# Summing a token's expert rows on TensorE, and layer 3 as one chain of stages per half of the tokens

## The chip, the core and the metric

The kernel runs on one core of a Trainium2 chip. The core has a matrix engine (TensorE; PE in the profile, PEld for its weight loads), a vector engine (VectorE, DVE), a scalar engine (ScalarE, ACT), a general engine (GpSimd, POOL), a queue for transfers (SyncE, SP) and 16 DMA engines. Each engine works through its own instructions in a fixed order and waits on semaphores for the others. Products land in PSUM, in eight banks; everything else lies in SBUF or in device memory. The metric is device microseconds for one execution.

## What is computed

The reference is a stack of four layers on 1024 tokens (x, 4 x 256 x 256, float32). Every layer is a feed-forward, an attention and the same feed-forward again, each on the normalized x and added to x. What matters here are layers 2 and 3:

```python
x = x + 0.5 * _L2_ffn_ref(_layernorm(x, axis=-1), ...)
x = x + _L2_attn_ref(_layernorm(x, axis=-1), ...)
x = x + 0.5 * _L2_ffn_ref(_layernorm(x, axis=-1), ...)
x = x + 0.5 * _L3_ffn_ref(_layernorm(x, axis=-1), ...)
x = x + _L3_attn_ref(_layernorm(x, axis=-1), ...)
x = x + 0.5 * _L3_ffn_ref(_layernorm(x, axis=-1), ...)
```

The feed-forward of layer 2 has 64 experts and a shared part. A token goes to its best six experts, and its output is the sum of their six rows and of the shared product:

```python
topk_w, topk_idx = jax.lax.top_k(scores, K)                    # K = 6 of E = 64
gx = xp[buf_tok]                                               # the tokens of each expert
hid = jax.nn.silu(g) * u                                       # gate and up, 96 wide
eo = jnp.einsum('ech,ehi->eci', hid, down_proj) * buf_w[..., None]
routed = jnp.zeros((T + 1, h), x.dtype).at[buf_tok.reshape(-1)].add(eo.reshape(-1, h))[:T]
shared = jax.nn.silu(xf @ shared_gate_w.T) * (xf @ shared_up_w.T) @ shared_down_w.T
return (routed + shared).reshape(b, s, h)
```

Layer 3's feed-forward is `relu(x @ w_up + b_up) @ w_down + b_down`, 256 to 1024 to 256. Its attention works on each of the four sequences of 256 tokens by itself: 16 query heads and 4 key heads with a rotary position, 16 tokens compressed into one key and one value by a softmax, a softmax of each query over the 16 compressed keys, and an output projection. Layer 3's feed-forward works token by token, so no token of one sequence needs another sequence.

## The kernel before

x stays in SBUF as eight tiles of 128 tokens (`m.x[0..7]`); tiles 0 to 3 are half 0 (two sequences), 4 to 7 half 1. `norm` (L165) makes statistics of each tile of a half on DVE (L172, L173), one inverse root for four tiles in a chain of 14 small DVE operations (`rsqrt`, L155 to L163), the normalized tile (`xn`, L180), two transposes per tile on PE with the identity (L136), and a copy into `xT[half]`, by turns on DVE (L142) and ACT (L144). `mm` (L132) is every chain of products, `add_to_x` (L204) adds a scaled result to x on DVE.

The program is written out in one order of tracing. A planner of the framework then orders each engine's instructions: it runs through its own simulated time, and each engine takes, of those instructions whose inputs are ready there, the one that was traced first. Where nothing is late the order on an engine is thus the order of tracing. Buffers of one name are handed out in rotation, in the order of tracing. A pool opened where an earlier pool lay waits until that one is free.

**Layer 2's feed-forward**, `l2_ffn`, is called twice, before and after layer 2's attention. It normalizes all eight tiles and then makes lists of tokens for the experts, mostly on DVE. In the second call `beside()` follows, which decodes layer 3's weights (PE, ACT, POOL). Then 16 groups of four experts run, up to eight at a time (`staggered`). A group gathers its tokens with two indirect transfers by POOL (L977, ten buffers named rows), transposes them, multiplies by gate and up (L996), makes h (L1006), multiplies by down and scatters the rows by two more indirect transfers by POOL (L1025) into `parts` in device memory, one row for each token and choice. The experts' weights come by SP in eight loads of gate and up and four of down, into six slots in the first call and five in the second. After the groups the shared part is traced: `gated` (L188 to L201) makes gate and up products of a half, 96 wide, into mmb banks, SiLU on ACT (L196) and the product on DVE (L198), and the down product of each tile goes to x (L204). Last, each tile of 128 tokens loads its 6 x 256 numbers per token from `parts` (`got`, L1043, four buffers, which waits for all scatters), POOL adds three of the six rows to the other three (L1049), and DVE adds the three to x (L204 again).

**Layer 3** is made of two generators, each of which traces a step and yields. `l3_ffn` (L1559) normalizes a half, adds the bias to x on POOL (L1563), yields, makes eight products of 512 columns (up, with ReLU by turns on ACT and DVE, L1572 and L1570) and yields after each, and then makes four tiles of the down product, each added to x. `l3_attn` (L1626) normalizes a half and then runs its two sequences in turns, the second three steps behind the first; a sequence has 18 steps, of products, rotary operations (L1646 on DVE, L1647 on POOL), two softmaxes (L1603 to L1610) and transposes. Both use mmb (four banks), trb (two) and accb (two). The main program runs the feed-forward of half 0 alone; then the attention of half 0 beside the feed-forward of half 1, two steps of attention to one of feed-forward; then the attention of half 1 beside the second feed-forward of half 0, in the same way; then the second feed-forward of half 1 alone. At the end SP stores each tile (L1793).

## Time and profile before

| | us |
|---|---|
| median of 14 runs | 2105.07 (2095.1 to 2111.15) |
| the profiled execution | 2095.62, its span 2093.9 |
| first layer-2 feed-forward: experts and their sums (first gather to the first product of the attention behind it) | 878.9 to 1006.6 |
| second layer-2 feed-forward: the same, to the first up-product of layer 3 | 1772.2 to 1894.3 |
| layer 3, first up-product to last add | 1894.3 to 2091.2 |
| busy: PE, DVE, ACT, POOL | 1815.4, 1199.3, 708.1, 577.7 |

Times are counted from the start of the span, in us. A line of a group or of the time line gives the engine, the line of the kernel, the operation, the tile written and the tiles read (`x<-got,x`), and the shape. What stands in square brackets is the time for which the engine had been idle, and what ended that. "x12924" counts instructions; a product of float32 is two records, each with a weight load. In the answers by stretches the columns are the length, the busy time and number of records of PE, PEld, DVE, ACT and POOL, the granted clock of TensorE as a share of its full speed, the mean share of the 16 DMA engines and GB/s.

### The profile page before, as it was taken

How to read it: one execution, taken by the hardware profiler on the slowest of the kernel's cores; microseconds unless marked ns; L12 is line 12 of the kernel's file. 1: busy time of each engine (PE TensorE's matmuls, PEld its weight loads, DVE VectorE, ACT ScalarE, POOL GpSimd, SP SyncE). 2: the span in 40 equal slices, each digit the busy share in tenths (PEclk: the TensorE clock that was granted, in tenths of full speed). 3: DMA queues.
4: the chain of work that ended last, by engine and by line, in shares of the span. 5: the costliest groups of instructions: out<-in, count | busy, mean ns of one | idle time of the engine just before them, and what ended most of it. 6: DMA issues, size and time to landing. Idle time of an engine off the chain costs nothing. (4 is left out here: it accounts for less than half of the span.)

```text
span 2093.9 us, 33727 instructions
## 1 busy us (share of the span) xinstructions
PE 1815.4 (87%) x12924; PEld 1184.0 (57%) x12924; DVE 1199.3 (57%) x2910; ACT 708.1 (34%) x1573; POOL 577.7 (28%) x1128
## 2 busy tenths in 40 slices
PE   3979999998998999487658999999999977877878
PEld 2445655466556566353346677667677754544546
DVE  8653434333555433545778887778675644464562
ACT  7325521101545201121324554545545532210220
POOL 0023200001323000176334435334333231761110
PEclk9976899999999999698769999999999985987999
DMA  8001002234000213295120111011011045960000
GB/s 232 3 10 41 11 19 61 86 108 165 1 1 1 82 41 81 85 297 194 48 82 22 42 42 51 32 52 37 17 37 37 16 108 149 290 211 0 1 0 21
DMA packets 121872, 147.38 MB, mean 70 GB/s; under 512 B 18008, under 2 KB 95472, under 8 KB 121712
## 3 DMA queue, kind: packets, MB, share of 16 engines
q1 hardware_dynamic: 113488, 123.72, 20.0%
q0 software_dynamic: 6144, 18.88, 2.9%
q8 instruction: 103, 1.69, 0.4%
q10 hardware_dynamic: 2080, 2.62, 0.3%
q14 instruction: 57, 0.47, 0.1%
HBM read 120.03 MB, written 25.17 MB: 69 GB/s over the span
## 5 line engine op out<-in xcount | busy, mean ns | idle before, releaser
L132 PE MATMUL mmb<-xT,slot 128*128 128x512 f32 (+2 forms) x640 | 285.6, 603 | 2.0 <-DVE h L198 1.0
L132 PEld LDWEIGHTS mmb<-xT,slot 128*128 128x128 f32 (+2 forms) x640 | 118.1, 188 | 151.7 <-issue 144.3
L204 DVE SCALAR_TENSOR_TENSOR x<-accb,x 128x256 f32<-128x256 f32 x112 | 47.0, 422 | 198.1 <-PE accb L132 197.9
L132 PE MATMUL accb<-slot,h 128*128 128x256 f32 (+2 forms) x640 | 145.3, 384 | 0.0
L132 PEld LDWEIGHTS accb<-slot,h 128*128 128x128 f32 (+2 forms) x640 | 118.9, 190 | 28.7 <-issue 13.9
L1181 DVE SCALAR_TENSOR_TENSOR qT<-mmb,l_conv,qT 128x510 f32<-128x510 f32 (+2 forms) x96 | 70.9, 738 | 60.3 <-ACT qT L1177 59.4
L596 ACT ACTIVATE sg<-mmb 128x512 f32<-128x512 f32 (+1 forms) x56 | 33.4, 597 | 199.2 <-PE mmb L132 196.3
L144 ACT COPY xT<-trb 128x256 f32<-128x256 f32 x44 | 16.4, 372 | 217.0 <-PE trb L136 191.2
L977 POOL DMA_INDIRECT rows<-table,source x64 | 61.9, 967 | 75.2 <-ACT l_ffn L1555 36.0
L778 POOL TENSOR_TENSOR e<-e,den 128x512 f32<-128x512 f32 x64 | 51.5, 827 | 109.4 <-DVE den L775 106.3
L1181 DVE SCALAR_TENSOR_TENSOR vT<-mmb,l_conv,vT 128x510 f32<-128x510 f32 (+2 forms) x96 | 71.2, 741 | 18.4 <-ACT vT L1177 17.5
L1227 POOL TENSOR_TENSOR put<-lt,t_same 32x128 f32<-32x128 f32 x128 | 63.9, 499 | 26.6 <-DVE lt L1222 19.8
L726 POOL TENSOR_TENSOR x<-x,l_bo 128x256 f32<-128x256 f32 x8 | 6.5, 834 | 230.7 <-DVE xn L180 230.7
L598 DVE TENSOR_TENSOR sg<-sg,c 128x512 f32<-128x512 f32 x44 | 30.9, 702 | 66.9 <-ACT sg L596 48.7
L1006 DVE SCALAR_TENSOR_TENSOR h<-sg,rows,mmb 64x96 f32<-64x96 f32 x128 | 40.1, 313 | 50.1 <-ACT sg L1001 47.9
L1025 POOL DMA_INDIRECT parts<-os,target x64 | 62.9, 984 | 19.5 <-issue 13.9
L1181 DVE SCALAR_TENSOR_TENSOR kT<-mmb,l_conv,kT 128x510 f32<-128x510 f32 (+2 forms) x96 | 66.5, 739 | 1.9 <-ACT kT L1177 1.7
L132 PE MATMUL mmb<-xT,wq 128*128 128x512 f32 x128 | 67.3, 650 | 0.0
L132 PE MATMUL accb<-wo,zT 128*128 128x256 f32 x256 | 61.7, 394 | 6.1 <-DVE x L204 4.5
L996 PE MATMUL mmb<-slot,gx 128*64 128x192 f32 x512 | 61.0, 358 | 6.4 <-DVE gx L142 5.8
L132 PE MATMUL mmb<-xT,l_ffn 128*128 128x512 f32 x128 | 63.5, 639 | 1.2 <-DVE xT L142 1.2
L132 PE MATMUL mmb<-xT,wv 128*128 128x512 f32 x128 | 63.7, 620 | 0.0
(452 smaller groups left out, 4307.1 us busy)
## 6 DMA issues: line engine op xcount, KB each, us to landing
slot<-_L_ffn_gate_up_proj_dram SPq DMA_DIRECT2D x16, 1536.0 KB, 14.4
slot<-in_L_ffn_down_proj_dram SPq DMA_DIRECT2D x8, 1536.0 KB, 17.7
parts<-zero SPq DMA_DIRECT2D x16, 768.0 KB, 9.7
got<-parts SPq DMA_DIRECT2D x16, 768.0 KB, 4.4
bca<-scr SPq DMA_DIRECT2D x32, 256.0 KB, 3.3
bcb<-scr SPq DMA_DIRECT2D x32, 256.0 KB, 3.4
c<-rows SPq DMA_DIRECT2D x16, 256.0 KB, 3.0
table<-xs ACTq DMA_DIRECT2D x2, 1280.0 KB, 5.1
```

The lines of the kernel that those rows point to most:

```text
L132: self.nc.tensor.matmul(out=out, lhsT=a, rhs=b, start=i == 0, stop=i == last, **kw)
L144: self.nc.scalar.copy(out, in_)
L204: self.nc.vector.scalar_tensor_tensor(self.x[t], got, scale, self.x[t], ALU.mult, ALU.add)
L596: nc.scalar.activation(sg[:n], g[:n], AF.Silu)
L598: nc.vector.tensor_tensor(sg, sg, c, ALU.mult)
L778: nc.gpsimd.tensor_tensor(e[:, :, cut], e[:, :, cut], den[:, i, :].unsqueeze(2).to_broadcast([P, 2, n]), ALU.mult)
L977: nc.gpsimd.indirect_dma_start(out=r, out_offset=None, in_=table, in_offset=bass.IndirectOffsetOnAxis(ap=slot[0][:, 2 * g + i : 2 * g + i ...
L996: nc.tensor.matmul(out=ps[half, i, :], lhsT=xT[:, i, k, half], rhs=gu[:, 4 * (g % 2) + 2 * i + j, k, :], start=k == 0, stop=k == KC - 1,)
L1006: nc.vector.scalar_tensor_tensor(h[half, i, :], sg[half, i, :], rows[i][half, D + e : D + e + 1], ps[half, i, 96:], ALU.mult, ALU.mult,)
L1025: ins = nc.gpsimd.indirect_dma_start(out=parts, out_offset=bass.IndirectOffsetOnAxis(ap=slot[1][:, 2 * g + i : 2 * g + i + 1], axis=0), in ...
L1181: nc.vector.scalar_tensor_tensor(yi[:, :, d:], ps[:, :, : S - d], tap(j), yi[:, :, d:], ALU.mult, ALU.add)
L1227: nc.gpsimd.tensor_tensor(batches[b].put[rows(q), :, :, u * G : u * G + G], lt[rows(q), :, rows(q)].rearrange("p c (z t) -> p t z c", z=2) ...
```

## The change

The shared part of layer 2's feed-forward is traced ahead of the experts, up to `h`, for both halves, and `h` is kept. Behind the experts each tile is one chain of products in one accb bank: the two of the shared down product and six more, each the identity times one of the six gathered rows, followed by one add to x. POOL's add and the three adds of rows on DVE are gone, and `got` has five buffers.

`norm` becomes a generator with one yield, between the inverse root and the normalizing; `norm` itself runs it through, and layer 3's two generators pass the yield on. In layer 3 each half is one chain: feed-forward, attention, feed-forward. The two chains run in turns, one step each, and half 1 starts when half 0 has made 14 steps.

```diff
     def norm(self, keep=None, halves=(0, 1)):
+        for _ in self.norm_steps(keep, halves):
+            pass
+
+    def norm_steps(self, keep=None, halves=(0, 1)):
...
             self.rsqrt(nc.vector, rs, step, v)
+            yield
             for q in range(4):
...
-def beside(a, b, each):
-
-    live = [a, b]
-    while live:
-        for g in list(live):
-            for _ in range(each if g is a else 1):
-                if next(g, live) is live:
-                    live.remove(g)
-                    break
...
         wk = pool("l2f", 2)
+        cols = lambda f: slice(f * 96, f * 96 + 96)
+        shared = [
+            m.gated(wk, half, lambda k, f: w.sg[:, k, cols(f)], lambda k, f: w.su[:, k, cols(f)], [96] * 2, "hs")
+            for half in range(2)
+        ]
         weights = {}
...
         staggered((experts(g) for g in range(16)), width=8, apart=1)
-        for half in range(2):
-            cols = lambda f: slice(f * 96, f * 96 + 96)
-            h = m.gated(wk, half, lambda k, f: w.sg[:, k, cols(f)], lambda k, f: w.su[:, k, cols(f)], [96] * 2, "hs")
-            for q in range(4):
-                o = m.acc_bank()
-                m.mm(o[:, :D], [(h[f][:96, q * P : (q + 1) * P], w.sd[:, f, :]) for f in range(2)])
-                m.add_to_x(half * 4 + q, o[:, :D], 0.5)
         for t in range(NT):
-            got = wk.tile([P, K, D], F32, name="got", bufs=4)
+            got = wk.tile([P, K, D], F32, name="got", bufs=5)
             ins = nc.sync.dma_start(
...
-            nc.gpsimd.tensor_tensor(got[:, :3], got[:, :3], got[:, 3:], ALU.add)
-            for k in range(3):
-                m.add_to_x(t, got[:, k], 0.5)
+            h, at = shared[t // 4], slice(t % 4 * P, t % 4 * P + P)
+            o = m.acc_bank()
+            m.mm(
+                o[:, :D],
+                [(h[f][:96, at], w.sd[:, f, :]) for f in range(2)] + [(m.ident, got[:, k]) for k in range(K)],
+            )
+            m.add_to_x(t, o[:, :D], 0.5)
...
 def l3_ffn(m, w, wk, half):
     nc = m.nc
-    m.norm(halves=(half,))
+    yield from m.norm_steps(halves=(half,))
...
     cos, sin, block, diag, cw, both = w.cos, w.sin, w.block, w.diag, w.cw, w.both
-    m.norm(halves=(half,))
+    yield from m.norm_steps(halves=(half,))
...
                     l3_attn_tables(m, wa, one)
-                    for _ in l3_ffn(m, w, wf, 0):
-                        pass
-                    beside(l3_attn(m, wa, wk, 0), l3_ffn(m, w, wf, 1), 2)
-                    beside(l3_attn(m, wa, wk, 1), l3_ffn(m, w, wf, 0), 2)
-                    for _ in l3_ffn(m, w, wf, 1):
-                        pass
+                    layer = lambda half: chain(
+                        l3_ffn(m, w, wf, half), l3_attn(m, wa, wk, half), l3_ffn(m, w, wf, half)
+                    )
+                    staggered((layer(half) for half in range(2)), 2, 14)
```

## The prediction

> **What bounds the kernel now.** I read the page first (span, engine shares), then the busy time by stretches, then the chain that ended last, and last the order of instructions in the two places that the change touches: each layer-2 feed-forward, and layer 3 from 1881 us on. The profiled execution took 2095.62 us around its span of 2093.9; the median of the 14 runs is 2105.07, 9.5 us above it. My sum is made against 2095.62, and the difference that it gives is put on the median.
>
> ```profile
> span 2093.9 us, 33727 instructions
> PE 1815.4 (87%) x12924; PEld 1184.0 (57%) x12924; DVE 1199.3 (57%) x2910; ACT 708.1 (34%) x1573; POOL 577.7 (28%) x1128
> ...
> 1771.00:1852.00 81.00, 65.47 (x483) 38.93 (x483) 33.50 (x88) 18.86 (x42) 59.48 (x61) 0.92 0.82 247
> ...
> 1861.60:1894.30 32.70, 18.16 (x48) 9.67 (x46) 29.00 (x61) 1.93 (x4) 18.13 (x12) 0.68 0.43 157
> 1894.28:1925.10 30.82, 30.82 (x96) 19.23 (x96) 6.11 (x13) 2.75 (x4) 0.00 (x0) 0.90 0.00 1
> 1925.10:1994.30 69.20, 56.53 (x225) 37.97 (x224) 40.71 (x134) 12.34 (x26) 9.96 (x16) 0.90 0.00 1
> 1994.30:2059.90 65.60, 52.95 (x226) 35.82 (x227) 44.05 (x152) 11.03 (x25) 11.49 (x18) 0.97 0.02 7
> 2059.90:2091.20 31.30, 29.08 (x105) 18.80 (x103) 6.83 (x13) 3.49 (x6) 1.45 (x2) 1.00 0.05 17
> ```
>
> After the length of a stretch come the busy times of PE, PEld, DVE, ACT and POOL, the granted clock, the DMA share and GB/s. PE bounds the kernel as a whole, but not here. In the experts (1771 to 1852) POOL has no room: its 64 gathers and scatters go out one per 1.27 us (0.97 busy, 0.30 of issue), 81 us. While the rows are summed (1861.6 to 1894.3) DVE is busy 29.0 of 32.7 us and PE 18.2. In layer 3 the two stretches with attention leave PE idle 12.7 us each.
>
> ```profile
> L204 DVE SCALAR_TENSOR_TENSOR x<-got,x x48: 399/425/2008, 971.4 to 1891.7; 128x256 f32<-128x256 f32 x48
> L1049 POOL TENSOR_TENSOR got<-got x16: 1790/1840/1998, 969.6 to 1882.4; 128x768 f32<-128x768 f32 x16
> ...
> 1772.21 1.08 POOL L977 DMA_INDIRECT rows<-table,source  x1 [35.99 <-ACT l_ffn L1555]
> 1778.48 2.71 PE L996 MATMUL mmb<-slot,gx 128*64 128x192 f32 x16
> 1851.78 1.96 PE L132 MATMUL mmb<-xT,l_sg 128*96 128x512 f32 x4
> 1857.25 21.05 SPq L1043 DMA_DIRECT2D got<-parts  x8
> 1861.64 1.80 POOL L1049 TENSOR_TENSOR got<-got 128x768 f32<-128x768 f32 x1 [5.92 <-DMA got<-parts]
> 1889.48 1.12 PE L136 MATMUL trb<-t_ident,xn 128*128 128x128 f32 x4 [3.77 <-DVE xn L180]
> 1894.28 17.02 PE L132 MATMUL mmb<-xT,l_ffn 128*128 128x512 f32 x32 [0.61 <-DVE xT L142]
> ...
> 1930.69 1.09 PE L136 MATMUL trb<-t_ident,xn 128*128 128x128 f32 x4 [5.58 <-DVE xn L180]
> 1941.18 1.88 PE L132 MATMUL mmb<-xT,l_ffn 128*128 128x512 f32 x4
> 2047.68 1.89 PE L132 MATMUL mmb<-l_attn,oT 128*128 128x256 f32 x8
> 2062.84 13.97 PE L132 MATMUL mmb<-xT,l_ffn 128*128 128x512 f32 x32 [0.61 <-DVE xT L142]
> ```
>
> To be seen: a DVE add of 0.42 us stretches to 2.0 beside a POOL add of 1.8; the experts' first gather waits for the last copy of layer 3's weights; the shared product runs in the pause between the last expert and the first rows; and 32 products of 512 columns take 17.02 us after a pause and 13.97 without one.
>
> **The sums on TensorE.** Removed per layer: 8 POOL adds of 1.84 us and 24 DVE adds (0.42 alone, 17.4 us busy in the second layer), with 8 adds of the shared product; 8 adds of 0.42 remain. Added: 8 x 6 products with the identity. A product in this precision is two records; 64 records of 256 columns take 13.98 us, 0.216 each, so a tile costs 16 records (4 shared, 12 identity), 3.46 us. The first two tiles' shared records fit before the rows land (two accb banks), so 120 records, 25.9 us, follow the first landing. Rows arrive faster (786 KB a tile at the 260 to 282 GB/s of this stage, 3.0 to 2.8 us), so PE sets the pace; the fifth got buffer and the SP queue, which has nothing behind these loads that is due, cost nothing.
>
> PE has been idle for 10 us by then (1851.8 to 1861.6), since the shared product that ran there has moved. The rows for a cold start are 7 records at 0.85 instead of 0.43 after 1894.28, and 4 at 0.85 after 1006.62: 3 or 1.7 us lost. I take 1.7, since a tile's records come without gaps. The Trainium skill, "TensorE: Matmul & The Clock Gate", Part 1, speaks against the move here: an idle window of about 3.4 us halves the clock, and about 3.4 us of activity restores it. By the page I estimate 1.7 us per start, and 3.4 where the activity straddles two windows; the granted clocks of 0.68 and 0.90 above agree that pauses lower it.
>
> First layer: landing at 969.59 plus 27.6 plus 0.3 gives x7's statistics at about 997.9, against 999.57: **-1.7 us** (between -4, DVE free of all its adds, and +2, a second cold window). Second layer: sums end at 1889.2. The norm of half 0 needs only tiles 0 to 3 (1876), its chain on DVE takes 4 to 5 us without the adds between, and its transposes (1.6 us on PE) lie among tiles 4 to 7. Up-products start at 1891 instead of 1894.28, on a warm clock: the feed-forward takes 27.8 (as at 2062.84) and not 30.8. **-6.3 us** (between -9 and -1, the transposes all behind the sums).
>
> **The shared product moved forward.** 32 records at 0.43 (1.88 for 4), 13.8 us warm and 27.2 cold, now traced ahead of the experts. Only 16 can go early: there are four mmb banks, and the next 16 wait for SiLU and product (0.59 and 0.68), whose buffers share memory that the routing and layer 3's weights free at 877.9 and 1771.95. Behind them on PE stand the experts' transposes and first products; behind those POOL, which has ten row buffers (12.7 us of gathers) before it waits for group 0. Second layer: 12 records from 1771.3, four of them cold, end at 1778.1; the next 16 at 1785; group 0's product, warm now (1.52, not 2.71), ends at 1786.6 against 1781.2, group 1's 4 us later than now. POOL runs dry for about 4 us: **+4** (between 0, idle PE covers it, and +20, all 32 cold). First layer: PE idles from 862 to 882 beside DVE's list building, so most is covered; group 0's product ends at about 891 against 889.3: **+2** (0 to +7). The later part of the experts is POOL's in both, so a late start is not won back.
>
> **Layer 3 in two chains.** No instruction is added; the order changes. A feed-forward has 14 steps and an attention 22, so half 1 starts with half 0's attention. From 1925.1 to 2091.2 it takes 166.1 us now. After:
> - attention 0 with feed-forward 1, 14 rounds. The norms behind the feed-forward still stand alone on DVE (5.6 us to the first transpose now), but half 1's transposes now come before most of the rotary work, so that its up-products start about 12.5 us in, not 16.1. Then 27.6 of feed-forward and 12 of attention (of 22 us of PE work per half: 52.95 less 27.6 and 3.2 of transposes), at what density? PE is busy 44.92 of the 50.3 us from 2009.6 to 2059.9, 89%; its waits for attention's results (r, kT, e, oT, aT, ck in the list of waits) are 10.3 us in the two stretches, and with one attention step, not two, between two feed-forward products I take half of them away: 94%. That makes 54.6, and 57 at 89%.
> - the last 8 steps of attention 0 beside the first of attention 1. Alone, those steps took 17.9 us (1966.45 to 1984.33): 18. DVE has some 24 us of work here (10.5 of attention 0, 6.5 of norm, 7 of attention 1) and can make it 27; with attention 1's share left for later, 16.
> - feed-forward 0 with the rest of attention 1: 9 for the norm, then 39 of PE work at 94%: 50.6.
> - feed-forward 1 alone. Attention 1 now ends in the round of feed-forward 0's last tile; today its last products (2047.68) leave three tiles, 10.5 us, to cover the norm, which costs 2.9. Uncovered: 1.9 of products, 8.4 of adds, statistics, root, transposes and copies, 1.7 cold, 27.8: 39.8 (31.3 if it stays covered).
>
> Sum 163.0, **-3.1 us**. Behind it stand only the output stores, as now.
>
> Total: -1.7 -6.3 +4 +2 -3.1 = -5.1: 2090.5 for a profiled run, **2100 at the median**, faster by 0.24%, at the edge of what a measurement of this kernel can tell from no change (about 0.2%, 4.2 us).
>
> **The rivals.**
> 1. Slower: the shared product holds up the experts. If its records stay cold (clock 0.50 from 1760 to 1780, and no dense work before), 28 take 23.8 us from 1771.3, and group 0 ends near 1796, not 1786.6; with 2 to 3 us more in the first layer the starts cost 18, and the total is +7: 2112. For it: the 2.71 us of the first expert products now. Against it: 32 products in a row are dense enough to end the cold state elsewhere within 6 us. It decides once both starts together lose over 15 us.
> 2. Slower: four sequences and a norm at once are too much for DVE (27 us, not 18), and four banks shared by three streams keep the density at 89% (+4.6). Total +8.5: 2113. For it: DVE is busy 44 of 65.6 us with two sequences. Against: attention 0 comes first in each round.
> 3. Clearly faster: PE's pauses at the norms are filled better than I grant. Attention 1 slips ahead by two rounds and covers the last norm (-8), or the experts' start costs nothing (-6): -12, 2093. For it: two joint norms of 11 to 16 us vanish from the middle. Against: the order of the banks holds steps near their round.
> 4. The move does nothing: the planner leaves the shared product where it has room, and the sums end as the adds did; only layer 3 moves, -3: 2102.
>
> **How the numbers follow.** Forecast 0.33 (own range 2094 to 2106; 0.2 of it below 2100.9), rivals 0.20, 0.20, 0.23 and 0.04. Faster by over 0.2%: 0.2 + 0.23 and 0.02 of the fourth, 0.45; within: 0.15; slower: 0.40. The range takes in the bounds: the starts' +20 and +7 less the gains at one end, the covered norm with the better tails at the other, 2083 to 2121.
>
> **What would show it.** Right: no POOL adds; first expert product of the second layer 4 us later after the last weight copy; 27 to 28 us from the first rows' landing to the last sum; up-products of layer 3 at 0.43 from their start; last feed-forward of 28 us after a pause of about 8. Wrong: POOL dry for over 10 us behind its tenth gather; over 24 us between feed-forward 1's end and the transposes of feed-forward 0's second norm; a PE pause under 4 us before the last feed-forward.

## The result and the profile after

The change makes the kernel slower. The median is 2128.49 us (2123.46 to 2133.98, 13 runs) against 2101.39 us for the kernel before (2092.73 to 2112.89, 62 runs, the 14 shown above among them): a ratio of 1.0130 with a 95% interval of 1.0115 to 1.0144, or +27 us. The prediction was 2100, with a range of 2083 to 2121.

The profiled execution after has a span of 2133.2 us, 39.3 more than the one before. That is more than the medians say, because before's profiled execution lay 5.8 us under the median of the 62 runs and after's 6.4 us over its own. The page of after, its span and its engines:

```profile
span 2133.2 us, 34022 instructions
PE 1868.6 (88%) x13116; PEld 1231.9 (58%) x13116; DVE 1167.0 (55%) x2862; ACT 707.5 (33%) x1573; POOL 547.4 (26%) x1112
```

PE has 192 records more, the products with the identity (2 feed-forwards x 8 tiles x 6 products x 2 records), and 53 us more of busy time; DVE and POOL have 32 and 30 us less. So the work moved as planned. The stages, each from its first instruction to the next stage's first:

| stage | before | after | difference |
|---|---|---|---|
| start to the first gather of layer 2 | 878.9 | 889.4 | +10.5 |
| layer 2, first feed-forward, to the first product of the attention | 127.7 | 134.3 | +6.6 |
| layer 2, attention, to the next norm's first transpose | 708.4 | 722.1 | +13.8 |
| norm and lists, to the second set of gathers | 57.2 | 54.9 | -2.3 |
| layer 2, second feed-forward, to the first up-product of layer 3 | 122.1 | 129.8 | +7.7 |
| layer 3, first feed-forward of half 0 | 30.8 | 27.8 | -3.0 |
| the rest | 168.8 | 174.8 | +6.0 |

The first and the third row are code that the change doesn't touch. Engine by engine, both profiles have the same instructions there in the same order, but for 2 and 16 records of TensorE among products that run side by side. The first row is a matter of the execution (last section); the third turned out to be the change's main cost.

The next lines are the busy time by stretches of the profile after (length; busy time and records of PE, PEld, DVE, ACT, POOL; clock; DMA share; GB/s), as the prediction showed them of before: the experts, the sums, and layer 3 in five parts.

```profile
1800.80:1890.10 89.30, 78.86 (x519) 44.72 (x518) 36.30 (x91) 20.44 (x45) 59.42 (x61) 0.96 0.76 224
1899.87:1930.60 30.73, 29.08 (x128) 24.80 (x129) 10.87 (x37) 0.74 (x2) 2.90 (x4) 0.95 0.43 167
1930.60:1958.40 27.80, 27.79 (x96) 18.13 (x96) 6.11 (x13) 2.75 (x4) 0.00 (x0) 1.00 0.00 1
1958.40:2011.21 52.81, 45.01 (x170) 28.80 (x171) 31.05 (x107) 9.91 (x20) 10.14 (x16) 0.90 0.00 0
2011.21:2049.16 37.95, 23.41 (x107) 15.81 (x105) 29.46 (x102) 7.29 (x18) 9.55 (x14) 0.83 0.00 1
2049.16:2089.30 40.14, 40.14 (x168) 27.71 (x168) 19.29 (x53) 6.31 (x13) 0.73 (x2) 0.95 0.03 10
2089.30:2130.40 41.10, 34.43 (x112) 21.43 (x111) 12.48 (x36) 3.49 (x6) 2.96 (x4) 0.88 0.04 13
```

To be seen: in the sums DVE fell from 29.0 to 10.9 us and PE rose from 18.2 to 29.1, so PE sets their pace; the feed-forward behind them runs on a full clock, 27.80 us instead of 30.82. (Three of the seven profiles with these sums on TensorE have 27.8 us there and four have 29.5; of seven without them 29.4 to 30.8. The mean gain is thus 1.3 us, not 3.) In layer 3 PE has no gap in the last row but one, and 14.5 us of idle time in the 37.95 us of the row above it, where no feed-forward runs.

The order of time in the second layer-2 feed-forward of after:

```profile
1799.71 3.62 PE L132 MATMUL mmb<-xT,l_sg 128*96 128x512 f32 x4
1803.12 2.44 PE L132 MATMUL mmb<-xT,l_su 128*96 128x512 f32 x4
1805.40 1.88 PE L132 MATMUL mmb<-xT,l_sg 128*96 128x512 f32 x4
...
1812.20 0.94 POOL L976 DMA_INDIRECT rows<-table,source  x1 [0.30 <-issue]
...
1817.10 2.81 PE L995 MATMUL mmb<-slot,gx 128*64 128x192 f32 x30
...
1820.42 0.94 POOL L976 DMA_INDIRECT rows<-table,source  x1 [7.28 <-DVE h L1005]
...
1899.87 7.09 PE L132 MATMUL accb<-got,t_ident 128*128 128x256 f32 x24 [9.75 <-DMA got<-parts]
1906.79 1.03 PE L132 MATMUL accb<-l_sd,hs 96*128 96x256 f32 x4
1907.66 2.75 PE L132 MATMUL accb<-got,t_ident 128*128 128x256 f32 x12
...
1930.60 13.97 PE L132 MATMUL mmb<-xT,l_ffn 128*128 128x512 f32 x32 [0.61 <-DVE xT L142]
```

All 32 records of the shared gate and up products run in front of the experts, 16.0 us from 1799.71 on; the first expert product comes 16.3 us after the first gather instead of 6.3, and POOL, its ten buffers full, waits 7.28 us for that group. The first rows are summed 9.6 us later after the first gather than before, and each tile takes 3.46 us.

The last lines are views around the attention of layer 2: the 20 us ahead of its first product, the whole of it, and the last 5 us ahead of it. First the kernel before, then after.

```profile
986.62:1006.62 20.00, 8.12 (x24) 4.97 (x25) 17.75 (x66) 1.12 (x3) 4.17 (x7) 0.50 0.15 44
1006.62:1714.99 708.37, 641.61 (x7529) 466.34 (x7529) 518.77 (x1094) 333.79 (x733) 268.45 (x738) 0.95 0.13 41
1001.62:1006.62 5.00, 2.13 (x8) 1.37 (x9) 3.68 (x16) 0.37 (x1) 0.00 (x0) 0.50 0.00 0
```

```profile
1003.73:1023.73 20.00, 14.82 (x69) 11.77 (x67) 11.90 (x48) 1.12 (x3) 0.27 (x5) 0.89 0.00 1
1023.73:1745.87 722.14, 650.32 (x7529) 473.11 (x7529) 518.60 (x1094) 333.46 (x733) 267.99 (x738) 0.94 0.13 40
1018.73:1023.73 5.00, 2.13 (x8) 1.37 (x8) 3.67 (x16) 0.37 (x1) 0.00 (x0) 0.54 0.00 0
```

The same 7529 records take 13.8 us longer. In the 20 us in front of them TensorE is busy with the sums, at a mean granted clock of 0.89 and not 0.50. In the last 5 us there is no such difference: the engines are busy for the same times, and the clock is 0.54 and 0.50.

### The profile page after: what moved, and what is told of

It is laid out like the page before. It is cut to its first block, busy times and chain, and to the rows that moved or that the text cites. A ratio compares the mean times of both kernels' runs of the same rounds, so it can differ in the third digit from the quotient of the medians.

```text
span 2133.2 us, 34022 instructions
## 1 busy us (share of the span) xinstructions
PE 1868.6 (88%) x13116; PEld 1231.9 (58%) x13116; DVE 1167.0 (55%) x2862; ACT 707.5 (33%) x1573; POOL 547.4 (26%) x1112
## 5 line engine op out<-in xcount | busy, mean ns | idle before, releaser
L144 ACT COPY xT<-trb 128x256 f32<-128x256 f32 x44 | 16.3, 371 | 220.7 <-PE trb L136 194.9
L132 PE MATMUL accb<-got,t_ident 128*128 128x256 f32 x192 | 48.5, 408 | 23.4 <-DMA got<-parts 23.4
L1024 POOL DMA_INDIRECT parts<-os,target x64 | 63.0, 984 | 22.8 <-issue 13.3
L592 DVE TENSOR_TENSOR sg<-sg,c 128x512 f32<-128x512 f32 x44 | 30.8, 701 | 67.0 <-ACT sg L590 43.7
```

The source lines that it names most:

```text
L132: self.nc.tensor.matmul(out=out, lhsT=a, rhs=b, start=i == 0, stop=i == last, **kw)
L592: nc.vector.tensor_tensor(sg, sg, c, ALU.mult)
L1024: ins = nc.gpsimd.indirect_dma_start(out=parts, out_offset=bass.IndirectOffsetOnAxis(ap=slot[1][:, 2 * g + i : 2 * g + i + 1], axis=0), in ...
```

## The experiments

Fifteen kernels ran, on three chips. On the first the kernel before takes 2101 to 2103 us, on the two others 2142 to 2147; the experts take longer there, at 181 GB/s among the first experts in l3_apart7's profile and 236 in the profile before. So every ratio is against the kernel before on the same chip, and of the times that were expected in the experiments of 2 to 4 only the differences count. A gain or loss in us is the ratio's, on the time before on that chip. All of them, with the length of the unchanged attention in the profile:

| kernel | ratio to before | interval | attention, us |
|---|---|---|---|
| layer 2's part alone (l2_only) | 1.0104 | 1.0073 to 1.0135 | 720.4 |
| layer 3's part alone (l3_only) | 1.0010 | 0.9986 to 1.0034 | 709.2 |
| TensorE sums, shared product left behind (sums_late) | 1.0068 | 1.0042 to 1.0094 | 725.5 |
| shared product ahead, old sums (early_old_sums) | 1.0017 | 0.9996 to 1.0037 | 705.6 |
| layer 2's part, first feed-forward (sums_first) | 1.0092 | 1.0068 to 1.0115 | 720.5 |
| layer 2's part, second feed-forward (sums_second) | 1.0007 | 0.9990 to 1.0024 | 708.0 |
| before, with unused products beside the first sums (warm_first) | 1.0121 | 1.0104 to 1.0138 | 720.7 |
| as sums_first, but only tiles 0 to 3 on TensorE (half_first) | 0.9981 | 0.9962 to 1.0000 | 708.4 |
| the changed kernel again (after_again) | 1.0082 | 1.0054 to 1.0110 | 721.1 |
| the changed kernel, first sums as in half_first (after_cold) | 0.9987 | 0.9965 to 1.0009 | 708.3 |
| shared product among the experts, second only (mid_second) | 0.9967 | 0.9944 to 0.9990 | 709.2 |
| layer 3 seven turns apart (l3_apart7) | 0.9917 | 0.9902 to 0.9931 | 705.7 |
| layer 3 fourteen apart, else the same (l3_pairs14) | 0.9989 | 0.9966 to 1.0011 | 709.0 |
| mid_second and l3_apart7 (both_best) | 0.9901 | 0.9869 to 0.9934 | 706.4 |
| both_best and half_first (best_cold) | 0.9906 | 0.9877 to 0.9935 | 705.1 |

**1. The parts alone.** Two kernels take one part each. The theory at this point: the loss is where the stage table has it, with the long attention either chance or a consequence of layer 2's part.

```diff
 l2_only, against the changed kernel (l3_ffn and l3_attn; main program):
-    yield from m.norm_steps(halves=(half,))
+    m.norm(halves=(half,))
...
-                    staggered((layer(half) for half in range(2)), 2, 14)
+                    for _ in l3_ffn(m, w, wf, 0):
+                        pass
+                    beside(l3_attn(m, wa, wk, 0), l3_ffn(m, w, wf, 1), 2)
+                    beside(l3_attn(m, wa, wk, 1), l3_ffn(m, w, wf, 0), 2)
+                    for _ in l3_ffn(m, w, wf, 1):
+                        pass
 l3_only, against the kernel before:
-                    beside(l3_attn(m, wa, wk, 0), l3_ffn(m, w, wf, 1), 2)
-                    beside(l3_attn(m, wa, wk, 1), l3_ffn(m, w, wf, 0), 2)
+                    staggered((layer(half) for half in range(2)), 2, 14)
```

> Layer 2's part of the change alone (shared product ahead of the experts, sums on TensorE, five got buffers), layer 3 as before. The two traces, compared stage by stage, put +6.6 us on the first layer-2 feed-forward, +7.8 on the second and -3.0 on the feed-forward behind it (warm clock): +11.4. Theory A (the stages compared are all there is, what is left of the +27 is the two profiled executions lying at opposite ends of their spreads, or layer 3): about 2113 against 2101.4. Theory B (the unchanged attention of layer 2, 11.4 us longer in the profile after, is lengthened by this part): about 2122. My prediction's terms for this part, -1.7 -6.3 +4 +2 = -2, would give 2099.

> Layer 3's part alone (one chain of stages per half, norm as steps), layer 2 as before. The traces put +6.0 us on layer 3 behind its first feed-forward. Theory A and B: about 2107, with some 38 us between the end of feed-forward 1 and the up-products of the second feed-forward 0. Rival C (layer 3 carries what the stages of layer 2 do not explain): 2117. My prediction's term of -3.1 would give 2098.

Measured: +22 us and +2 us. For layer 3's part no loss can be told (-3 to +7 us); nearly all of it is layer 2's. l2_only came out near theory B's 2122 (2127.6, before 2103.4 beside it), and its attention took 720.4 us. Rival C falls.

Two more kernels split layer 2's part, both against l2_only.

```diff
 sums_late:
-        shared = [
-            m.gated(wk, half, lambda k, f: w.sg[:, k, cols(f)], lambda k, f: w.su[:, k, cols(f)], [96] * 2, "hs")
-            for half in range(2)
-        ]
...
         staggered((experts(g) for g in range(16)), width=8, apart=1)
+        shared = [
+            m.gated(wk, half, lambda k, f: w.sg[:, k, cols(f)], lambda k, f: w.su[:, k, cols(f)], [96] * 2, "hs")
+            for half in range(2)
+        ]
 early_old_sums:
         staggered((experts(g) for g in range(16)), width=8, apart=1)
+        for half in range(2):
+            h = shared[half]
+            for q in range(4):
+                o = m.acc_bank()
+                m.mm(o[:, :D], [(h[f][:96, q * P : (q + 1) * P], w.sd[:, f, :]) for f in range(2)])
+                m.add_to_x(half * 4 + q, o[:, :D], 0.5)
...
-            m.mm(
-                o[:, :D],
-                [(h[f][:96, at], w.sd[:, f, :]) for f in range(2)] + [(m.ident, got[:, k]) for k in range(K)],
-            )
-            m.add_to_x(t, o[:, :D], 0.5)
+            nc.gpsimd.tensor_tensor(got[:, :3], got[:, :3], got[:, 3:], ALU.add)
+            for k in range(3):
+                m.add_to_x(t, got[:, k], 0.5)
```

> The sums on TensorE with five got buffers, but the shared product where it was, behind the experts; layer 3 as before. Theory A: the experts start and end as before; the shared gate and up products fill the pause until 1869.5 us of the profile before, 8 us past the first landing, and 128 records of 0.216 follow: sums end at about 1897 against 1892.1, +5 per layer, less 3 for the first feed-forward of layer 3 on a warm clock: about 2108. Rival D (moving the shared product costs nothing, the sums on TensorE themselves are what is slow): as slow as layer 2's part alone. Rival E (sums as fast as predicted, hidden beside the shared product): 2093 to 2097.

> The shared product ahead of the experts alone; the six rows are summed by POOL and DVE as before, four got buffers, layer 3 as before. Theory A: the experts end 5.8 and 9.7 us later as in the profile after, and the sums behind them are shorter by the shared adds and products that DVE no longer has there, 2 us per layer: +11, about 2112. Rival D (the early product is free): 2097 to 2101.

Measured: +14 us (9 to 20) and +4 us (-1 to +8). Theory A fits neither; rival D touches both intervals, at their edges. The product ahead of the experts did start them late (their last product came 5.5 and 7.7 us later after the first gather), but the sums behind it had DVE and TensorE for themselves: the first attention began only 3.3 us later after the first gather than before, and the first up-product of layer 3 1.2 us later after the lists. What is slow goes with the sums on TensorE, wherever the shared product stands. Yet nothing in the sums themselves is slow: from the first landing to the attention's first product it is 37.0 us before and 37.8 after, from the second landing to the up-products 32.6 and 30.7. What the kernels with TensorE sums had in common was the long attention.

**2. What lengthens the attention.** Three kernels: layer 2's part in the first feed-forward only, in the second only, and the kernel before with TensorE kept busy, by products that nobody reads, while POOL and DVE do the first sums.

```diff
 sums_first, against the kernel before (l2_ffn_new is the changed l2_ffn):
-                    l2_ffn(m, w2, tables[0])
+                    l2_ffn_new(m, w2, tables[0])
 sums_second:
-                    l2_ffn(m, w2, tables[1], lambda: late.extend((l3_ffn_weights(m), l3_attn_weights(m))))
+                    l2_ffn_new(m, w2, tables[1], lambda: late.extend((l3_ffn_weights(m), l3_attn_weights(m))))
 warm_first, against the kernel before, in the first l2_ffn only:
+            o = m.acc_bank()
+            m.mm(o[:, :D], [(m.ident, got[:, 3 + k % 3]) for k in range(6)])
             nc.gpsimd.tensor_tensor(got[:, :3], got[:, :3], got[:, 3:], ALU.add)
```

> Layer 2's part of the change in its first feed-forward only; the second and layer 3 as before. In three profiles with TensorE sums the unchanged attention of layer 2 took 738 to 743 us from its first product of the decays to the router of the next feed-forward's list, in three without them 723 to 729. Theory F (the sums in front of it lengthen the attention): +3 to +6 from the feed-forward's late start, +10 to 14 in the attention: 2115 to 2121 against 2103, and 738 to 743 us in the profile. Rival G (the attention's length is chance of an execution, the loss lies in the second feed-forward): 2105 to 2109, 723 to 729.

> Layer 2's part of the change in its second feed-forward only. Theory F: the attention in front is as before (723 to 729 us); the second feed-forward's late start, less its shorter sums and the warm clock behind them, +4 to +8: 2107 to 2111. Rival G: it carries most of layer 2's +24: 2118 to 2124. My prediction's terms for it, +4 and -6.3: 2101.

> As before, with six unused products of 256 columns per tile on TensorE beside the old sums of the first feed-forward of layer 2 (they read the three rows that POOL doesn't write); nothing waits for them but the buffer of the rows. Nothing of the computation is left out. Theory F1 (a TensorE that comes into the attention at full clock is what lengthens it): 735 to 743 us for the attention, 2111 to 2117. Rival F2 (it is something else of the sums on TensorE, or chance): 723 to 729 us, 2101 to 2106.

Measured: +19.7 us, +1.5 us and +26 us. The loss is in the first feed-forward and what follows it; in the second the change is neutral. The unused products alone lengthen the attention to 720.7 us. The first two of the views above, of warm_first:

```profile
1020.78:1040.78 20.00, 15.46 (x70) 12.32 (x69) 17.54 (x45) 1.12 (x3) 5.63 (x7) 0.87 0.21 74
1040.78:1761.49 720.71, 646.07 (x7529) 469.42 (x7529) 517.16 (x1094) 333.82 (x733) 269.78 (x738) 0.94 0.13 40
```

DVE does the sums here (17.54 of 20 us, as before), and still the attention is 12 us longer. The clock of 0.87 is again the mean of 20 us; over the last 5 it is 0.50. The total of warm_first was missed: its first feed-forward took 161.9 us as well, against 151.1 in l3_apart7 on the same chip; that the unused products hold the got buffers longer is likely, but wasn't tried.

The opposite edit: TensorE sums, but a pause in front of the attention, by giving tiles 4 to 7 back to POOL and DVE.

```diff
 half_first, against sums_first:
+            summed = [(m.ident, got[:, k]) for k in range(K)] if t < 4 else []
-            m.mm(
-                o[:, :D],
-                [(h[f][:96, at], w.sd[:, f, :]) for f in range(2)] + [(m.ident, got[:, k]) for k in range(K)],
-            )
+            m.mm(o[:, :D], [(h[f][:96, at], w.sd[:, f, :]) for f in range(2)] + summed)
             m.add_to_x(t, o[:, :D], 0.5)
+            if t >= 4:
+                nc.gpsimd.tensor_tensor(got[:, :3], got[:, :3], got[:, 3:], ALU.add)
+                for k in range(3):
+                    m.add_to_x(t, got[:, k], 0.5)
```

> In the first feed-forward of layer 2 the shared product ahead of the experts and TensorE's sums for tiles 0 to 3; tiles 4 to 7 are summed by POOL and DVE as before, so that TensorE pauses before the attention. The rest as before. If the clock at which TensorE enters the attention decides (theory F1): the attention takes 705 to 709 us, not 720, and the kernel lies 0 to +8 us from before. If it is the sums on TensorE as such, or the shared product ahead of the experts: 713 to 721 and +10 to +20.

Measured: 708.4 us for the attention, and the kernel 0.19% under before, 0.9962 to 1.0000, where sums_first is 0.92% over.

```profile
1017.80:1037.80 20.00, 9.54 (x42) 6.93 (x40) 17.02 (x69) 1.12 (x3) 4.59 (x8) 0.71 0.13 42
1037.80:1746.20 708.40, 642.70 (x7530) 467.25 (x7529) 519.02 (x1094) 333.71 (x733) 268.92 (x738) 0.95 0.13 40
```

PE is idle for half of the 20 us in front. So the long attention needs neither the shared product ahead of the experts, which warm_first leaves behind, nor sums that anything reads. Theory F1 in its own words, a TensorE that comes in at full clock, does not stand: over the last 5 us in front the clock is 0.50 to 0.54 in all seventeen profiles. Two things remain, and they go together in every kernel. Those with the long attention have no pause of TensorE over 3.6 us in the 20 us in front, and 96 records more on TensorE ahead of it (8 tiles x 6 products x 2). Those with the short one have a pause of 7 us or more there, and 48 records more or none. The ratios cannot part the two; the next section's traces tell more.

**3. The same edit in the changed kernel.** One question was left: is this what makes the whole change slower, or do neutral parts lose time together?

```diff
 after_cold, against the changed kernel (l2_ffn_half is half_first's):
-                    l2_ffn(m, w2, tables[0])
+                    l2_ffn_half(m, w2, tables[0])
```

> The changed kernel itself once more, beside the next one on the same chip: 1.1 to 1.5% slower than before, its attention of layer 2 at 720 to 723 us.

> The changed kernel with one edit: in the first feed-forward of layer 2 the rows of tiles 4 to 7 are summed by POOL and DVE again, so that TensorE pauses before the attention. The second feed-forward and layer 3 stay changed. If TensorE's full clock at the attention's start is what made the change slower: the attention takes 705 to 709 us and the kernel is within 0.3% of before, 0.8 to 1.3% under the changed kernel. If the rest of the change carries part of it (second feed-forward +1.6 us and layer 3 -1 to +2 by the runs of each alone): at most 0.5% over before. Rival (several places lose a little each): 0.6% or more over before.

Measured on one chip: 2163.59 and 2139.50 us. The one edit takes 24 us off by the medians, 20 by the ratios, and brings the changed kernel to before's level (0.9987). The change itself cost less on this chip (1.0082) than on the first, under the range expected. The longest waits of PE in the attention (who waited for whom; us in total, times, the longest), first of after_again, then of after_cold:

```profile
PE mmb L132 <- DVE inv L1261: 13.8, 2, 10.0
PE accb L132 <- DVE u L1398: 10.8, 14, 2.1
PE mmb L132 <- issue: 9.9, 6, 2.8
```

```profile
PE mmb L132 <- DVE inv L1445: 13.4, 2, 9.6
PE accb L132 <- DVE u L1582: 9.6, 13, 1.2
PE mmb L132 <- issue: 5.5, 4, 3.4
```

Of the 12.8 us, PE is busy for 6.0 longer (648.56 against 642.60 for the same records: 87 us of the attention are at half clock, not 68) and idle for 6.8 longer. That is the difference in waits for nothing that the profile names ("issue"): 12.3 us against 5.5 over all of TensorE's products, 9.9 against 5.5 in the group shown.

These waits have fixed places. TensorE has 4023 records ahead of the attention in the eight kernels that add none, 4071 in the three with half of the first sums, 4119 in the six with all of them or as many unused products. The first long wait inside the attention of before is in front of its record 458; in half_first of record 411; in after of record 364. Counted from the start of the program, that is behind 4479 to 4483 records in all seventeen profiles. In this order, with after's next wait and the only transfer in the 3.2 us around that one (1084.6 to 1087.8):

```profile
1068.71 0.23 PE L132 MATMUL mmb<-xs,inv 32*32 32x16 f32 x1 [3.15 <-issue]
1099.55 0.23 PE L132 MATMUL mmb<-xs,inv 32*32 32x16 f32 x1 [3.62 <-issue]
1084.08 0.28 PE L132 MATMUL mmb<-inv,xs 32*32 32x16 f32 x5 [2.80 <-issue]
1087.81 0.53 PE L132 MATMUL mmb<-inv,lt 32*32 32x32 f32 x12 [1.80 <-issue]
...
q8 instruction: 1, 0.02, 2.3%
```

The transfer is a packet of 16 KB on a queue for instructions (103 such packets move 1.69 MB in before's profile), and it ends 1.4 us before TensorE goes on. Of the waits over 0.7 us in the seventeen attentions, all but a short one at record 56 end 1.2 to 1.5 us after the end of such a packet. They lie whole multiples of about 126.6 records apart (128, 1391, 2405, 1267 and 759 in after). So TensorE waits there for its own instructions, which come in pieces, and products added ahead move the attention against the ends of the pieces. With 96 records more the waits add up to 11.9 to 13.1 us and the half clock to 80 to 94 us; with 48 or none, to 4.6 to 6.9 and 61 to 71. In after_again the half clock begins as such a wait ends at 135, 394 and 565 us into the attention. A kernel that adds the records and keeps the pause was not run, so a part of the pause in it is not excluded.

Of the rest, the first feed-forward is 6.8 us shorter (148.4 against 155.2): with half of the tiles on each, DVE and TensorE share the sums, and from the first rows' sum to the attention it is 33.3 us, not 37.4. Together that is 19.6 us, about the 20 of the ratios.

**4. Layer 3, and a version that beats both.** In the joint stretch of after (2011 to 2049) these are the longest waits of PE, with the same columns:

```profile
PE trb L136 <- DVE xn L185: 8.0, 4, 4.6
PE mmb L132 <- DVE e L1606: 3.2, 1, 3.2
PE trb L136 <- DVE r L1645: 2.3, 2, 1.5
```

Norms that no feed-forward covers. l3_apart7 starts half 1 in the middle of half 0's feed-forward, so that dense products lie beside every norm but those of the middle; l3_pairs14 has its two steps to a turn without the early start.

```diff
 l3_apart7, against l3_only (l3_pairs14 keeps the 14):
+                    def pairs(steps):
+                        while next(steps, wk) is not wk and next(steps, wk) is not wk:
+                            yield
                     layer = lambda half: chain(
-                        l3_ffn(m, w, wf, half), l3_attn(m, wa, wk, half), l3_ffn(m, w, wf, half)
+                        l3_ffn(m, w, wf, half), pairs(l3_attn(m, wa, wk, half)), l3_ffn(m, w, wf, half)
                     )
-                    staggered((layer(half) for half in range(2)), 2, 14)
+                    staggered((layer(half) for half in range(2)), 2, 7)
```

> Layer 2 as before; layer 3 as one chain per half, the attention two steps to a turn, and half 1 started seven turns behind half 0 instead of fourteen. If the loss of the changed layer 3 is the norms that no feed-forward covers (14.6 us of TensorE idle between feed-forward 1 and the second feed-forward 0, 8 before feed-forward 1): the first of these pauses goes, the middle one has the second half of feed-forward 1 in front and the first of feed-forward 0 behind: 8 to 20 us less than before, 2083 to 2095. Rival (DVE bounds the middle, since four sequences and two norms meet there): 2100 to 2110.

> Layer 2 as before; layer 3 as in the kernel started seven turns apart, but fourteen apart, so that the attention takes eleven turns of two steps. It tells the start from the two steps. If the start of half 1 in the middle of half 0's feed-forward is what gained 18 us: -4 to +5 us from before, with both pauses for the norm of 8 to 16 us back. Rival (two steps a turn gain it): -12 to -18.

Measured: 0.9917, 18 us less than before, and 0.9989. The two steps alone gain nothing that can be told; the early start gains it, though it was run with the two steps only. Layer 3 of l3_apart7, in stretches (the last is the whole):

```profile
1934.62:1973.12 38.50, 38.24 (x121) 23.11 (x122) 11.59 (x30) 4.76 (x8) 2.97 (x4) 0.93 0.00 0
1973.12:2009.24 36.12, 33.77 (x147) 22.54 (x146) 23.64 (x76) 8.06 (x16) 7.25 (x12) 1.00 0.00 1
2009.24:2049.34 40.10, 26.80 (x121) 18.39 (x119) 30.23 (x109) 8.03 (x20) 9.12 (x14) 0.82 0.00 0
2049.34:2079.34 30.00, 29.91 (x118) 19.05 (x119) 22.06 (x72) 6.28 (x13) 3.76 (x6) 0.95 0.00 1
1934.62:2121.14 186.52, 167.23 (x648) 110.64 (x648) 93.92 (x297) 29.88 (x61) 23.11 (x36) 0.94 0.02 6
```

PE is idle for 19.3 of 186.5 us, 13.3 of them in the stretch of 40 us between the feed-forwards, which is about as long as in the changed kernel (37.95, 14.5 idle). In the kernels with before's order layer 3 takes 199 to 207 us from its first up-product.

The last part is the second feed-forward of layer 2 with the shared product where TensorE has room.

```diff
 mid_second, in the second l2_ffn only:
+            if g in (6, 10):
+                piece(0, (g - 6) // 4)        # gate, up, SiLU and product: half 0, one 96 wide
...
         staggered((experts(g) for g in range(16)), width=8, apart=1)
+        for f in range(2):
+            piece(1, f)
```

> In the second feed-forward of layer 2 TensorE sums, with the shared product of half 0 in two pieces among the experts (behind the gate and up products of groups 6 and 10) and that of half 1 in the pause behind the last expert; the first feed-forward and layer 3 as before. The experts start as early as before. If the late start of 8 to 10 us is what ate the gain of the sums in the second feed-forward alone (ratio 1.0007): 4 to 8 us less than before. Rival (the pieces push the later groups back by as much as the early product did): within 3 us of before.

> The first feed-forward of layer 2 as before, the second with the shared product among the experts and TensorE sums, and layer 3 with half 1 started seven turns behind. If the parts add up: -18 from layer 3 and -4 to -8 from the second feed-forward, 1.0 to 1.25% under before. Rival (layer 3's early second half wants the DVE time that the sums leave anyway, and the gains overlap): -18.

> All that gained: half of the first sums on TensorE (-0.19%), the second sums with the shared product among the experts (-0.33%), and layer 3 with half 1 started seven turns behind (-0.83%). If they add up: 1.2 to 1.4% under before. Rival (the sums' gains were within the spread): 0.8 to 1.0%.

Measured: 0.9967 for mid_second (-7 us, as expected; its last expert product came 102.4 us after the first gather, against 101.2 in l3_pairs14 on the same chip), 0.9901 for both_best and 0.9906 for best_cold. The first two parts gain 0.33% and 0.83% alone and 0.99% together (0.66 to 1.31), which fits their sum and the rival's 0.83 as well. The halved first sums bring nothing more that can be measured: best_cold's 0.94% lies under the 1.2 to 1.4 expected and in its rival's range. both_best beats both kernels, before by 21 us (14 to 28) by its ratio.

## Why the prediction was wrong

**The missing term.** The sum counted only the stages that the change touches: two feed-forwards and layer 3. "Total: -1.7 -6.3 +4 +2 -3.1" has no term for the attention between them, which was left out and so put at nothing, without a reason given. It took 12 to 14 us more, half of the +27. In place of that nothing, the runs showed that it takes as much more with 96 records added ahead of it on TensorE, the sums' or unused ones, and that half of them cost it nothing. The traces show where the time goes: waits of TensorE for its instructions, 12.1 us in after's attention against 6.3 in before's, and 88 us at half clock against 64. None of the four rivals had it either.

The prediction weighed the Trainium skill, "TensorE: Matmul & The Clock Gate", Part 1, only for the cold starts that the move makes. The page's closing section ("Why this matters for your kernels") advises against pauses of TensorE of over about 3 us. Here the kernels with a pause of 7 us or more in front of the attention are the faster ones in it; since they also have fewer records ahead, no run shows that this is the pause's doing, and nothing here speaks against the advice. The page also says that the clock halves after an idle window of about 3.4 us; in sums_first and after_cold, between 105 and 205 us into the attention, it was halved behind windows of that length in which PE was 29 to 70% busy by its records.

**The sums.** Right in kind and pace: no POOL adds, PE sets the pace, 3.46 us a tile, up-products of layer 3 at 0.44 from the start. First layer: forecast -1.7 from the landing to the attention, measured +0.8. The term that was too small is the cold start: 24 records took 8.4 us there, not 5.2, and 3.2 us were lost instead of 1.7; the last sum came 29.1 us after the landing, not 27.6. (The terms of that line add up to 997.5, not 997.9.) Second layer: forecast -6.3, measured -4.9 (-1.9 to the up-products, -3.0 in the feed-forward, of which 1.3 is left in the mean of the profiles).

**The shared product moved forward.** Forecast +2 and +4, measured +5.8 and +9.6 at the landings, within the bounds of 0 to 7 and 0 to 20. The term that was too small is what stands ahead of the second layer's first expert product. Counted were 28 records, four of them cold, which put that product about 12.9 us behind the first gather (1785 against 1772.2). It was all 32 in a row, six of them cold, and behind them transposes and two records of the shared down product: 16.3 us, and POOL waited 7.28 us, not about 4. Rivals 1 and 2 (2112 and 2113) had the direction. Rival 1 had not the mechanism: the records were at full clock from the seventh on, and POOL waited 7 us, not over 10. The two starts lose 15.4 us together, just past the point from which rival 1 was to decide; yet the product ahead of the experts with the old sums costs 4 us (early_old_sums, interval -1 to +8), because what moves forward is gone from the sums' stage.

**Layer 3.** Forecast -3.1, measured 1.0010 for the part alone, no difference that can be told. Of its stages, attention 0 beside feed-forward 1 came out as worked out (52.8 us, forecast 54.6), the last feed-forward with its norm too (41.1, forecast 39.8). The step that failed is the middle: 18 us for the last steps of attention 0 and 9 for the norm behind them, 27 in all, took 38. The sign to look for, over 24 us between feed-forward 1's end and the transposes of feed-forward 0's second norm, was there (34.1 us). DVE has 29.5 us of work in it, near the 27 named as its bound: four sequences and two norms. That the norms' chains wait for each other's turns is likely, but wasn't tried. Rival 2's density of 89% is not what happened: beside a feed-forward PE was 100% busy. And the base was too low: from the end of the first feed-forward to the end, the profile before took 168.8 us, and eight other profiles with the same order 171 to 177 (mean 174); the four with the changed order took 173.5 to 174.8. One profile's stage is not a stage's time; the spread of layer 3 is as large as the gain that I read into it.

**The account.** Against the kernels without the edit, the profile after has +14.4 us in the attention (mean of three on the same chip 707.7), +6.6 in the first feed-forward, +4.7 in the second and the feed-forward behind it, +0.6 in the rest of layer 3 (174.8 against the mean of 174.2): 26.3 of the 27. (The norm and lists are left out: they take 54.9 or some 57 us in kernels of both kinds.) That it comes so near is partly luck, since single profiles of one stage differ by 1 to 3 us. Single runs of parts agree: +22 for layer 2, +2 for layer 3.

The delay does not arise in one place. after_again against after_cold is 1.8 us late 70 us into the attention, 5.1 at 140, 10.1 at 400 and 13.2 at 566, and in front of each step after_again has a wait for instructions (its records 492, 1251, 4288 and 6314). Two courses, 705 to 709 and 720 to 726 us, are shown by seventeen profiles without one in between. What stays open is why some ends of pieces hold TensorE up and most do not, and what the pause in front adds, if anything.

## What to carry to other kernels

A change that adds products to TensorE also moves every later stage against the pieces in which its instructions come, and an untouched stage of many small products may run on another course: put a term with a range on it, look at where its "issue" waits lie, and test it by taking half of the added products out or by adding unused ones. When work is taken off a busy engine, try half of it: from the first rows to the attention it took 33 us with half of the tiles on TensorE, 35 to 37 with none and 36 to 38 with all, though the whole kernel's gain is at the edge of what can be told (0.9962 to 1.0000). Before two halves of a token stream are staggered, lay out which dense stage covers each norm; here a start in the middle of a dense stage, not at its end, was worth 18 us, with two attention steps to a turn.

## What the runs showed of the hardware

An attention of 7529 records on TensorE takes 705 to 709 us with 0 or 48 records added ahead of it and 720 to 726 with 96. TensorE's waits of 0.7 to 4.2 us for its own instructions in it lie behind the same number of records from the start of the program in all profiles, or whole multiples of about 126.6 further on, and end 1.2 to 1.5 us after a packet of 16 KB on a queue for instructions.

The first 880 us, which no kernel here touches, end at 877.6 to 880.7 us in twelve profiles and at 888.8 to 889.9 in five. In the profile after, a long one, TensorE has the half clock for 17 us from 251 on, where before has it for 3 and, at 259, for 7, and at six later places up to 610 us, where before has it at one. The times of one kernel can fall in two groups that would fit this, though no run shows that it is the reason: l2_only took 2121 to 2123 us at a mean clock of 0.919 to 0.921 and 2132 to 2133 at 0.913 to 0.915. A profile's time must be set against the median of its kernel before stages are compared; here it was worth 12 of the 39 us between the two profiles.

The same kernel took 2101 to 2103 us on one chip and 2142 to 2147 on two others, with 78 to 84 and 100 to 104 us from the first gather to the last expert product of its first feed-forward, the kernels with the shared product ahead among them.
